# A two-layer graph network on one core: a fourth buffer for the streamed weight, the identity in a borrowed tile, the scale folded into a weight product, and one pair of input loads asked for a stage later

## The chip, the cores and the metric

The kernel runs on one NeuronCore of a Trainium2 chip. The core has five engines that run side by side and are synchronised by semaphores only: TensorE (PE in the profile, with its weight loads as PEld), VectorE (DVE), ScalarE (ACT), GpSimd (POOL) and SyncE (SP). SP computes nothing; it issues DMA transfers, one after the other, in the order in which the program lists them. The metric is device time in microseconds (us) for one execution; shown is the median of several runs.

## The reference, cut to what matters

There are 32 graphs ("batches") of 512 nodes with 512 features, in float32. For each batch two layers are applied:

```python
# layer 0
h = relu(layernorm(x))
agg = (adj @ h) / max(rowsum(adj), 1e-6)
x = x + relu(concat([h, agg]) @ W.T)
# layer 1
h = relu(layernorm(x))
q, k = split(h @ Wqk);  v = h @ Wv
agg = adj @ (k * mask[:, None])
w = (1 / sqrt(512)) * mask * rowsum(q * agg)
x = x + softmax(w over the nodes)[:, None] * v
```

Every one of the large products is 512x512x512. W, Wqk and Wv are the same for all batches.

## The kernel before, in words

**Products.** Every 512x512 product is cut into 2x2 blocks of 256x256 and done by the Strassen-Winograd scheme: seven block products instead of eight, with sums and differences of blocks made beforehand by DVE (`left_sums`, `right_sums`) and afterwards by DVE and ACT out of PSUM (`finish`, `copy`). `ORDER` (L82) lists the order of the seven block products. `product` (L118) is a generator: it gives control back after every group of matmuls, so that other work can be issued between the groups.

**Stages.** Layer 1's score needs only q . (A k), so the kernel forms M = Wq Wk^T once and multiplies h M by A (mask h). W's halves are W1, for h, and W2, for the aggregate. For each batch i the main loop (L851) runs four stages on PE:

- O, `layer0_out(i)`, 14 steps: h W1 plus A (h W2). Step 2j is the W1 term of the j-th block product, step 2j+1 its adjacency term.
- TV, `layer1_tv(i-1)`, 14 steps: the product of the previous batch's h1 with the packed weight `mv` (M and Wv side by side), in two levels of the block scheme.
- U, `layer1_u(i)`, 7 steps: the adjacency times the masked h1.
- Y, `layer0_y(i+1)`, 7 steps: h W2 of the next batch.

**Order of the other work.** The whole order is written by hand: a `Plan` says after which step of a stage a function is issued (`p.at(step, function)`), and `run` (L167) walks through the steps. Each engine then works off its own instructions strictly in this order. SP does the same with its DMA issues: a transfer that has to wait for a buffer or for another transfer holds back everything that is behind it in SP's list.

**W1's slots.** `wide` holds W2's blocks and h; W1's seven block sums don't fit beside them and lie in DRAM (`dw`). `Stream.load` (L406) brings one of them, 256 KB, into a slot of the pool `w1` (three slots, L408), and each is read by one step of O. In before three loads are asked for at step 0 of U (L959) and the other four at steps 1, 3, 5 and 7 of O (L859); a load in O waits until PE has read the slot that it takes over.

**The fronts.** For each batch, two batches ahead, x and adj are loaded in halves into the tag `n`, which has two slots in all (`half_tile`, L199). `FrontH.load` loads a half of x, `stats` (DVE), `variance` (DVE and POOL), `shift` (DVE) and `write` (ACT, then SP) normalise it and write it to DRAM (`dhT`), and `to.read` reads it back in another order (`shT`) for a transpose on DVE. `FrontA` does the same with adj (`sum` on ACT for the row sums, `degrees` on DVE, `write` on ACT and SP to `daT`, `to.read` as `saT`, `turn` on DVE). The slots are shared: the x of batch 4 can be loaded only when the adj of batch 3 has been scaled and written out of them. From batch 3 on, x of the batch after next is asked for in U (L984) and Y (L1032). The first batches have an order of their own: x of batch 4 is asked for in steps 5 and 6 of Y(2) (L1029, L1030).

**Scale and mask.** `mask_keep` (L787) makes two tiles out of the transposed node mask: `mraw`, the mask, and `mcol`, the mask times 1/sqrt(512). `factor` (L337, POOL) multiplies the row sums of adj by `mcol`, and the score is multiplied by that (`scores`, L543). `place` (L810, ACT) copies the blocks of M and of Wv into `mv`.

**The identity.** PE transposes with an identity matrix in a tile of its own (`identity`, L218, 128x128). `late` (L688) is a tile with 6272 columns that the start uses for Wq, Wk and the mask, in its first 5120 columns, and whose slot later holds `h1T`.

Of the kernel before, what the change touches and what calls it, by code (L numbers as in the profile page):

```python
# [11 lines left out]
F32 = mybir.dt.float32  # L12
AF = mybir.ActivationFunctionType
ALU = mybir.AluOpType
AX = mybir.AxisListType

P = 128
# [5 lines left out]
def kernel(  # L23
# [35 lines left out]
    nc = tc.nc  # L59
    B, N, F = x.shape  # L60
    C = N // P
    H = F // 2
# [36 lines left out]
    def copy(o, i):  # L99
        nc.scalar.activation(o, i, AF.Copy)  # L100
# [114 lines left out]

    mhalf = const.tile([P, C], F32, name="mhalf")
    nc.vector.memset(mhalf, -0.5)
    identity = const.tile([P, P], F32, name="identity")  # L218
    make_identity(nc, identity)

    X, AT_, DEG, W, Y, H1M, H1T, U, TV = ({} for _ in range(9))

# [3 lines left out]
    def load_x(b):  # L226

        t = xu_tile(f"xu_{b}")
        X[b] = t.rearrange("p (c f) -> p c f", c=C)
        U[b] = t.rearrange("p (k i f) -> p k i f", k=4, i=2)  # L230
        load_rows(X[b], x[b])
# [82 lines left out]
    class FrontA:  # L314
# [21 lines left out]

        def factor(self):  # L337
            W[self.b] = small.tile([P, C], F32, tag="wd", bufs=3, name=f"wd_{self.b}")
            nc.gpsimd.tensor_tensor(W[self.b], DEG[self.b], mcol[:, :, self.b], op=ALU.mult)

        def write(self, c):
            v = self.n[c // 2][:, c % 2, :]
# [55 lines left out]
    class Stream:  # L398
# [6 lines left out]

        def load(self):  # L406
            k = ORDER[self.n % 7]
            t = big.tile([P, 2, H], F32, tag="w1", bufs=3, name=f"w1_{self.n}")  # L408
            nc.sync.dma_start(out=t, in_=self.d[RIGHT[k]])
            self.tiles.append((k, t))  # L410
            self.n += 1
# [204 lines left out]
        else:  # L616
            nc.vector.transpose(dst[:, :, ts(h, H)].rearrange("p a (k r) -> p k a r", r=R), t)

    mcol = const.tile([P, C, B], F32, name="mcol")
    mraw = const.tile([P, C, B], F32, name="mraw")  # L620

    def in_order(t):
# [6 lines left out]
    held = {}  # L629

    def turn_chunk(src, c, name):

        p = held[name, c] = mm_tile(f"{name}_{c}").rearrange("p a f -> p (a f)")
        for k in range(C):
            nc.tensor.transpose(p[:, ts(k, P)], src[:, ts(k, P)], identity)

    def keep_chunk(dst, c, name, by=copy):
        by(
# [29 lines left out]

    def start():

        load_x(0)
        s2 = [exchange(weight_source(w0[:, F:2 * F])[8 * h:8 * h + 8], f"sw2_{h}") for h in range(2)]
        fa = FA[0] = FrontA(0)
# [11 lines left out]
            fh.load(h, room[:, 9728 + 1024 * h:9728 + 1024 * (h + 1)].rearrange("p (c f) -> p c f", c=2))  # L685
        sq = exchange(weight_source(wqk[:, 0:F]), "swq", rows16(5632))
        sk = exchange(weight_source(wqk[:, F:2 * F]), "swk", rows16(7680))
        late = big.tile([P, 7, 7, P], F32, tag="h1T", bufs=1, name="late").rearrange("p s i f -> p (s i f)")  # L688
        wqT = late[:, 0:2048].rearrange("p (c f) -> p c f", c=C)
        wkT = late[:, 2048:4096].rearrange("p (c f) -> p c f", c=C)  # L690
        mask_sb, mask_by = late[:B, 4096:4608], late[:B, 4608:5120]
# [36 lines left out]
        p = Plan()  # L728
# [56 lines left out]
                nc.tensor.transpose(m[:, c, :], mask_by[:, ts(c, P)], identity[:B, :B])  # L785

        def mask_keep():  # L787
            nc.scalar.activation(mcol, held["pmk"], AF.Copy, scale=scale)
            nc.scalar.activation(mraw, held["pmk"], AF.Copy)

        p.at(8, mask_order)
        f = F1[0] = FrontH1(0)
# [15 lines left out]
                )  # L808

        def place(d, which, src):  # L810
            copy(
                mv[:, 2 * (d // 2):2 * (d // 2) + 2, 2 * (d % 2):2 * (d % 2) + 2, which, :],
                src.rearrange("p (a b f) -> p a b f", a=2, b=2),
            )

        def outer(s):
# [31 lines left out]
    with tc.manual_schedule(engines=engines):  # L848
        weights, mvR = start()
        post = None  # L850
        for i in range(B):  # L851
# [4 lines left out]
            if i > 0:  # L856

                p = Plan()
                for n in range(4):  # L859
                    p.at(2 * n + 1, stream.load)  # L860
                right_y = right_sums(of(Y[i]))
                p.at(0, right_y[0])
                p.at(0, right_y[2])
                for k in (1, 3):
                    p.at(2 + 2 * (k // 2), FA[i].sums, k)
                    p.at(2 + 2 * (k // 2), right_y[k])
                if i == 1:
                    for k, g in enumerate(weights[4:]):
                        p.at(3 + 2 * k, g)
                    fa = FA[2]  # L870
                    for h in range(2):
                        for c in range(2):
                            p.at(2 + 2 * h + c, fa.sum, 2 * h + c)
                            p.at(8 + 2 * h + c, fa.write, 2 * h + c)
                        p.at(5 + 2 * h, fa.degrees, h)
                    FH[3] = FrontH(3)
                    p.at(12, FH[3].load, 0)
                    p.at(13, FH[3].load, 1)
                f1 = F1[i - 1]
                for k in range(4):  # L880
                    p.at(k // 2, f1.sums, k)
                if post is not None:
                    for c in range(C):
                        p.at(2 + c, post.apply, c)
                    p.at(3, post.add_x1, 0)
                    p.at(5, post.add_x1, 1)
                    p.at(9, post.store, 0)
                    p.at(11, post.store, 1)
                for k in range(4):
                    p.at(2 + k, f1.inner_sums, k, 0, 7)  # L890
                if 1 < i and i + 2 < B:
                    fh = FH[i + 2]
                    for c in range(C):
                        p.at(3 + c, fh.stats, c)
                        p.at(10 + c, fh.write, c)
                    p.at(7, variance, fh.t)
                    p.at(9, shift, fh.t)
                if more:
                    th = FH[i + 1]
                    p.at(2, th.to.read, 1)  # L900
                    p.at(11, th.turn, 0)
                if 1 < i and i + 2 < B:
                    fa = FA[i + 2] = FrontA(i + 2)
                    p.at(12, fa.load, 0)
                p.at(12, f.stats, 0)
                p.at(12, f.stats, 1)
                p.at(13, variance, f.t, 0, 2)
                run(layer0_out(i, stream.take), 14, p)


                post = Post(i - 1, F1[i - 1])
                p = Plan()
                p.at(0, f.stats, 2)
                p.at(0, shift, f.t, 0, 2)
                p.at(0, f.stats, 3)
                p.at(1, variance, f.t, 2, 4)
                if last:
                    p.at(1, FA[i].factor)
                p.at(3, shift, f.t, 2, 4)
                for c in range(C):  # L920
                    p.at([2, 3, 5, 6][c], f.write, c)
                    p.at(8 + c, f.mask, c)
                p.at(1, f.keep)
                for k in range(4):
                    p.at([10, 12, 12, 12][k], f.masked_sums, k)
                if 1 < i and i + 2 < B:
                    p.at(1, fa.load, 1)
                    for h in range(2):
                        for c in range(2):
                            p.at(4 + 4 * h + 2 * c, fa.sum, 2 * h + c)  # L930
                        p.at(8 + 4 * h, fa.degrees, h)
                if i == 1:
                    fa = FA[3] = FrontA(3)
                    p.at(11, fa.load, 0)
                    p.at(13, fa.load, 1)
                    fh = FH[3]
                    for c in range(C):
                        p.at(4 + c, fh.stats, c)
                        p.at(9 + c, fh.write, c)
                    p.at(7, variance, fh.t)  # L940
                    p[9].insert(0, lambda t=fh.t: shift(t))
                if more:
                    p.at(3, th.turn, 1)
                    for k in range(4):
                        p.at(5 + k // 2, th.sums, k)
                p.at(8, f.to.read, 0)
                p.at(9, f.to.read, 1)
                for k in range(7):
                    p.at(12 + k // 4, post.recombine, k, 0, 0)
                run(layer1_tv(i - 1), 14, p)  # L950
# [3 lines left out]
            if more:  # L954
                p.at(0, f.turn, 0)
                p.at(1, f.turn, 1)
                p.at(2, FA[i + 1].to.read, 0)
                p.at(3, FA[i + 1].to.read, 1)
                for n in range(3):  # L959
                    p.at(0, stream.load)  # L960
            if i == 0:
                fh = FH[2]
# [35 lines left out]
            if more:  # L998
# [17 lines left out]
                if i == 0:  # L1016
                    for c in range(C):
                        p.at([2, 3, 4, 4][c], fh.write, c)
                    for k in range(1, 4):
                        p.at(3 + k, weights[k])  # L1020
                    FA[2] = FrontA(2)
                    p.at(5, FA[2].load, 0)
                    p.at(6, FA[2].load, 1)
                elif i == 1:
                    p.at(0, fa.degrees, 1)
                    for c in range(C):
                        p.at(2 + c, fa.write, c)
                    FH[4] = FrontH(4)
                    p.at(5, FH[4].load, 0)  # L1029
                    p.at(6, FH[4].load, 1)  # L1030
                elif i + 3 < B:
                    p.at(0, FH[i + 3].load, 1)  # L1032
                run(layer0_y(i + 1), 7, p)
# [74 lines left out]
```

## Time and profile before

| what | value |
|---|---|
| median of 7 runs | 2293.31 us (2289.42 to 2294.66) |
| the profiled execution | 2293.65 us |
| its span, first to last instruction | 2291.6 us |
| PE busy | 2247.8 us, 98% of the span |
| DVE busy | 1930.9 us, 84% |
| ACT busy | 1027.5 us, 45% |
| POOL busy | 185.8 us, 8% |
| bytes moved | 463.65 MB, 202 GB/s on average |

The profile counts a PE matmul as busy while it is in the array, so 98% says that matmuls were nearly always under way, and not how fast they ran. How fast is said by the granted clock (PEclk, 1.00 is full speed). "Idle before, releaser" is the time in which an engine had nothing under way just before an instruction, and the work whose end let that instruction start. Durations of DMA issues on SP (SPq) are those of the issue; when the data has arrived is given as the time to landing.

### The profile page before, as it was taken

How to read it: one execution, taken by the hardware profiler on the slowest of the kernel's cores; microseconds unless marked ns; L12 is line 12 of the kernel's file. 1: busy time of each engine (PE TensorE's matmuls, PEld its weight loads, DVE VectorE, ACT ScalarE, POOL GpSimd, SP SyncE). 2: the span in 40 equal slices, each digit the busy share in tenths (PEclk: the TensorE clock that was granted, in tenths of full speed). 3: DMA queues.
4: the chain of work that ended last, by engine and by line, in shares of the span. 5: the costliest groups of instructions: out<-in, count | busy, mean ns of one | idle time of the engine just before them, and what ended most of it. 6: DMA issues, size and time to landing. Idle time of an engine off the chain costs nothing.

```text
span 2291.6 us, 32519 instructions
## 1 busy us (share of the span) xinstructions
PE 2247.8 (98%) x10372; PEld 1970.1 (86%) x10372; DVE 1930.9 (84%) x3807; ACT 1027.5 (45%) x1901; POOL 185.8 (8%) x267
## 2 busy tenths in 40 slices
PE   7998999999999999999999999999999999999996
PEld 6787888888888888888888888888888888888885
DVE  6797888888888888888888888888888888888868
ACT  4454434544434454444454345444344544444332
POOL 0000000000100000100000000000000001000002
PEclk9999999999999999999999999999999999999998
DMA  9877877777878777778878777878787778777552
GB/s 220 231 215 207 214 201 202 209 221 200 215 193 210 214 217 206 212 191 210 222 205 215 202 198 211 222 197 220 191 211 210 219 204 215 190 210 209 152 138 65
DMA packets 409594, 463.65 MB, mean 202 GB/s; under 512 B 37680, under 2 KB 271152, under 8 KB 405328
## 3 DMA queue, kind: packets, MB, share of 16 engines
q1 hardware_dynamic: 400176, 428.56, 68.5%
q0 software_dynamic: 8928, 32.51, 8.3%
q8 instruction: 82, 1.34, 0.3%
q14 instruction: 88, 0.72, 0.1%
q10 hardware_dynamic: 320, 0.52, 0.1%
HBM read 293.93 MB, written 167.51 MB: 201 GB/s over the span
## 4 chain that ended last, share of the span: by engine, by line
PE 95%; DMA 2%; DVE 2%; SPq 0%; issue 0%; ACT 0%; DVEq 0%; POOL 0%; ACTq 0%
PE ptv L467 28%; PE pp_o L130 19%; PE pq_o L130 10%; PE pp_y L130 9%; PE pp_u L130 9%; PE pq_u L130 5%; PE pq_y L130 5%; PE pr_o L130 5%; PE pr_y L130 2%; PE pr_u L130 2%; DVE wide L94 1%; PE pm L805 1%; DMA a<-in_adj_dram 1%; DMA late<-in_nodemask_dram 0%; DMA w<-dw 0%; DVE tv L94 0%
## 5 line engine op out<-in xcount | busy, mean ns | idle before, releaser
L467 PE MATMUL ptv<-mv,h1T 128*128 128x256 f32 x3136 | 682.8, 379 | 1.4 <-DVE h1T L97 1.2
L467 PEld LDWEIGHTS ptv<-mv,h1T 128*128 128x128 f32 x3136 | 595.6, 190 | 83.4 <-DVE h1T L97 1.6
L94 DVE TENSOR_TENSOR tv<-tv 128x256 f32<-128x256 f32 (+1 forms) x644 | 321.6, 511 | 11.6
L100 ACT ACTIVATE tv<-ptv 128x512 f32<-128x512 f32 (+1 forms) x372 | 191.3, 541 | 285.2 <-PE ptv L467 283.8
L130 PE MATMUL pp_o<-y,aT 128*128 128x256 f32 x1024 | 241.9, 379 | 0.0
L130 PE MATMUL pp_y<-wide 128*128 128x256 f32 x1024 | 241.9, 379 | 0.0
L130 PE MATMUL pp_u<-h1m,aT 128*128 128x256 f32 x1024 | 241.9, 379 | 0.0
L130 PE MATMUL pp_o<-w,wide 128*128 128x256 f32 x992 | 234.3, 379 | 0.0
L130 PEld LDWEIGHTS pp_u<-h1m,aT 128*128 128x128 f32 x1024 | 194.6, 190 | 26.9 <-issue 0.5
L130 PEld LDWEIGHTS pp_o<-y,aT 128*128 128x128 f32 x1024 | 194.5, 190 | 26.4
L130 PEld LDWEIGHTS pp_y<-wide 128*128 128x128 f32 x1024 | 194.5, 190 | 26.3
L130 PEld LDWEIGHTS pp_o<-w,wide 128*128 128x128 f32 x992 | 188.5, 190 | 25.6
L100 ACT ACTIVATE o<-pp_o 128x512 f32<-128x512 f32 x96 | 57.3, 597 | 296.8 <-PE pp_o L130 296.8
L94 DVE TENSOR_TENSOR tv<-ptv,tv 128x512 f32<-128x512 f32 x248 | 144.7, 614 | 46.4 <-PE ptv L467 42.5
L100 ACT ACTIVATE y<-pp_y 128x512 f32<-128x512 f32 x128 | 76.3, 596 | 234.7 <-PE pp_y L130 233.4
L97 DVE TENSOR_TENSOR h1T<-h1T 128x512 f32<-128x512 f32 (+2 forms) x195 | 168.0, 875 | 1.2
L100 ACT ACTIVATE xu<-pp_u 128x512 f32<-128x512 f32 x128 | 76.4, 597 | 198.0 <-PE pp_u L130 198.0
L248 POOL TENSOR_TENSOR rstd<-rstd,mhalf 128x2 f32<-128x2 f32 (+1 forms) x96 | 78.4, 817 | 656.9 <-DVE rstd L247 656.9
L94 DVE TENSOR_TENSOR tv<-ptv,m_tv 128x512 f32<-128x512 f32 (+1 forms) x124 | 74.5, 622 | 63.9 <-PE ptv L467 62.6
L130 PE MATMUL pq_o<-w,wide 128*128 128x256 f32 x496 | 119.2, 384 | 6.9 <-DMA w<-dw 6.9
L130 PE MATMUL pq_o<-y,aT 128*128 128x256 f32 x512 | 121.8, 381 | 0.0
L130 PE MATMUL pq_y<-wide 128*128 128x256 f32 x512 | 121.0, 379 | 0.0
(112 smaller groups left out, 3173.1 us busy)
## 6 DMA issues: line engine op xcount, KB each, us to landing
w<-dw SPq DMA_DIRECT2D x217, 256.0 KB, 4.2
xu<-in_x_dram SPq DMA_DIRECT2D x128, 256.0 KB, 5.5
a<-in_adj_dram SPq DMA_DIRECT2D x256, 128.0 KB, 3.1
dh1T<-h1m SPq DMA_DIRECT2D x128, 256.0 KB, 3.1
dx<-xu SPq DMA_DIRECT2D x32, 1024.0 KB, 5.0
sh1T<-dh1T SPq DMA_DIRECT2D x256, 128.0 KB, 3.4
shT<-dhT SPq DMA_DIRECT2D x248, 128.0 KB, 4.4
daT<-a SPq DMA_DIRECT2D x124, 256.0 KB, 3.0
```

The source lines that it names most:

```text
L94: (on or nc.vector).tensor_tensor(o, a, b, op=ALU.add)
L97: (on or nc.vector).tensor_tensor(o, a, b, op=ALU.subtract)
L100: nc.scalar.activation(o, i, AF.Copy)
L130: nc.tensor.matmul(p[:, rc, :], lt[:, LEFT[k], dk, ts(rc, P)], right[:, dk, :], start=first and n == 0, stop=True, skip_group_check=True,)
L248: nc.gpsimd.tensor_tensor(rstd[:, a:b], rstd[:, a:b], mhalf[:, a:b], op=ALU.pow)
L467: nc.tensor.matmul(banks[n][:, :, ts(i, P)], left[:, LEFT[k], LEFT_IN[j], :], mvR[:, RIGHT[k], RIGHT[j], :, :], start=first and i == 0, st ...
L805: nc.tensor.matmul(m.rearrange("p a f -> p (a f)"), wqT[:, a, ts(d, P)], wkT[:, a, :], start=(a == 0), stop=(a == C - 1),)
```

## The change

Four edits go together.

1. `identity` is no longer a tile of its own; it lies in columns 5120 to 5247 of `late`, which is therefore allocated at the beginning of `start`.
2. `mcol` is gone. `factor` multiplies by the unscaled mask, and the factor 1/sqrt(512) is applied by `place` when M is copied into `mv`; `mask_keep` makes one tile instead of two.
3. The pool `w1` has four slots. Four loads are asked for at step 0 of U and three at steps 1, 3 and 5 of O. The second half of the read-back of the next h (`th.to.read(1)`) goes from step 2 to step 4 of O.
4. x of batch 4 is asked for at steps 1 and 3 of O(2), between the loads of W1, instead of steps 5 and 6 of Y(2). Its statistics go from steps 3 to 6 to steps 5 to 8 of O(2), and the variance from step 7 to step 8.

```diff
-    identity = const.tile([P, P], F32, name="identity")
-    make_identity(nc, identity)
...
-            nc.gpsimd.tensor_tensor(W[self.b], DEG[self.b], mcol[:, :, self.b], op=ALU.mult)
+            nc.gpsimd.tensor_tensor(W[self.b], DEG[self.b], mraw[:, :, self.b], op=ALU.mult)
...
-            t = big.tile([P, 2, H], F32, tag="w1", bufs=3, name=f"w1_{self.n}")
+            t = big.tile([P, 2, H], F32, tag="w1", bufs=4, name=f"w1_{self.n}")
...
-    mcol = const.tile([P, C, B], F32, name="mcol")
...
+        late = big.tile([P, 7, 7, P], F32, tag="h1T", bufs=1, name="late").rearrange("p s i f -> p (s i f)")
+        identity = held["identity"] = late[:, 5120:5248]
+        make_identity(nc, identity)
         load_x(0)
...
-            nc.scalar.activation(mcol, held["pmk"], AF.Copy, scale=scale)
-            nc.scalar.activation(mraw, held["pmk"], AF.Copy)
+            copy(mraw, held["pmk"])
...
-            copy(
+            nc.scalar.activation(
                 mv[:, 2 * (d // 2):2 * (d // 2) + 2, 2 * (d % 2):2 * (d % 2) + 2, which, :],
-                src.rearrange("p (a b f) -> p a b f", a=2, b=2),
+                src.rearrange("p (a b f) -> p a b f", a=2, b=2), AF.Copy, scale=1.0 if which else scale,
             )
...
                 p = Plan()
-                for n in range(4):
+                for n in range(3):
                     p.at(2 * n + 1, stream.load)
...
                     fh = FH[i + 2]
+                    late = 0
+                    if i == 2:
+                        late = 2
+                        p.at(1, fh.load, 0)
+                        p.at(3, fh.load, 1)
                     for c in range(C):
-                        p.at(3 + c, fh.stats, c)
+                        p.at(3 + late + c, fh.stats, c)
                         p.at(10 + c, fh.write, c)
-                    p.at(7, variance, fh.t)
+                    p.at(7 + late // 2, variance, fh.t)
                     p.at(9, shift, fh.t)
                 if more:
                     th = FH[i + 1]
-                    p.at(2, th.to.read, 1)
+                    p.at(4, th.to.read, 1)
...
-                for n in range(3):
+                for n in range(4):
                     p.at(0, stream.load)
...
                     FH[4] = FrontH(4)
-                    p.at(5, FH[4].load, 0)
-                    p.at(6, FH[4].load, 1)
```

More of the change, by code (lines that the diff above doesn't have):

```diff
@@ L634, in turn_chunk @@
         for k in range(C):
-            nc.tensor.transpose(p[:, ts(k, P)], src[:, ts(k, P)], identity)
+            nc.tensor.transpose(p[:, ts(k, P)], src[:, ts(k, P)], held["identity"])
     def keep_chunk(dst, c, name, by=copy):
@@ L687, in start @@
         sk = exchange(weight_source(wqk[:, F:2 * F]), "swk", rows16(7680))
-        late = big.tile([P, 7, 7, P], F32, tag="h1T", bufs=1, name="late").rearrange("p s i f -> p (s i f)")
         wqT = late[:, 0:2048].rearrange("p (c f) -> p c f", c=C)
```

## The prediction

> **What bounds the kernel now.** I read the page first (busy shares, granted clock), then PE's waits, then the chain of waits around the longest of them, then windows and DVE's timeline there.
>
> ```profile
> PE 2247.8 (98%) x10372; PEld 1970.1 (86%) x10372; DVE 1930.9 (84%) x3807; ACT 1027.5 (45%) x1901; POOL 185.8 (8%) x267
> PEclk9999999999999999999999999999999999999998
> ```
>
> PE is busy for 98% of the span at nearly full clock, so time can be won only where PE stands still or runs slowly. These are all of PE's waits:
>
> ```profile
> PE h L635 <- ACT h L707: 13.6, 1, 13.6
> PE pq_o L130 <- DMA w<-dw: 6.9, 1, 6.9
> PE pq_o L130 <- ACT m_o L100: 1.5, 1, 1.5
> PE ptv L467 <- DVE h1T L97: 1.2, 1, 1.2
> PE ptv L467 <- DVE xu L94: 0.2, 1, 0.2
> ```
>
> The first and third lie in the start, the last two in the last batch, the second in batch 2. PE's windows from one O to the next, of batches 1, 2 and 3, with PE busy, granted clock, DMA share and GB/s:
>
> ```profile
> 95.41:164.88 69.47, 69.47 (x322) 1.00 0.71 193
> 164.88:244.29 79.41, 72.52 (x324) 0.96 0.84 216
> 244.29:313.79 69.50, 69.50 (x323) 1.00 0.80 209
> ```
>
> A batch takes 69.5 us with PE never idle; batch 2 takes 79.41, 9.91 more, in which the 6.89 us wait is only a part. The chain through it:
>
> ```profile
> 171.95 1.58 PE pp_o L130 x8
> 173.54 8.62 DMA w<-dw
> 182.16 0.14 issue
> 182.30 6.31 PE pq_o L130 x16
> 188.60 3.45 PE pp_o L130 x16
> ```
>
> PE is done with the third block product of O(2) at 175.41 and waits until 182.30 for the fourth block of W1, whose transfer was issued at 173.54 and took 8.62 us. The next 16 matmuls take 6.31 us instead of 3.45: in 182.30 to 188.44 the granted clock is 0.57. Why the transfer is issued so late stands in SP's timeline:
>
> ```profile
> 150.42 2.33 SPq L409 DMA_DIRECT2D w<-dw  x3
> 152.80 4.35 SPq L212 DMA_DIRECT2D saT<-daT  x8
> ...
> 167.05 0.34 SPq L344 DMA_DIRECT2D daT<-a  x1
> 168.20 5.24 SPq L204 DMA_DIRECT2D n<-in_x_dram  x8
> 173.54 0.37 SPq L409 DMA_DIRECT2D w<-dw  x1
> 174.01 3.19 SPq L212 DMA_DIRECT2D shT<-dhT  x4
> 177.29 9.10 SPq L409 DMA_DIRECT2D w<-dw  x3
> ```
>
> The load takes a slot that PE frees at about 166.7 (O(2)'s first step), but on SP it stands behind eight loads of x of batch 4, which had to wait until batch 3's adj was written out (167.05) and keep SP until 173.44. The program puts this only into batch 2.
>
> **The change part by part.**
>
> *Fourth slot, four loads in U.* The block that PE waits for becomes the last of the w loads at about 152.7, 22 us before its use at 175.4; the longest landing of a w in this stretch is 8.9 us. The wait goes: -6.89. With it goes the slow clock behind it: 6.31 - 3.45 = -2.86. The remaining 0.13 is the next stage's first product group (21.29 against 21.15 elsewhere, seen in batch 1 too); I take 0 of it. Sum -9.75. Here a rule can be weighed. The Trainium skill, "TensorE: Matmul & The Clock Gate", section "What's actually happening", says that an idle array drops to half clock and comes back after a busy window of about 3.4 us. By that the slow clock would be worth an estimated 1.7 us (half of 3.4) and the sum -8.6; the row here has 2.86.
>
> *What is late next among the w loads.* Three remain in O(2), at steps 1, 3, 5, now between the x loads. A step lasts 24.17 / 14 = 1.73 us, O(2) starts at 164.88, so they are needed at steps 8, 10 and 12: 178.7, 182.2 and 185.6. SP is free after 167.4; w, four x (2.6 us), w, four x, four shT (3.2) and w then go out at about 168, 171 and 177.3, each after PE freed its slot (166.7, 170.1, 173.5). With this stretch's 8.6 us they land at 176.6, 179.6 and 185.9; with the all-over median of 4.2, four us sooner. The third is 0.3 late at worst. I take 0, since 0.75 MB of the traffic that made 8.62 then lies in front of it and has landed; bounds 0 and 0.3.
>
> *One more load in front of saT (U).* The extra w costs SP 0.4 to 0.8 us (three took 2.33), and its 256 KB at the 236 GB/s of this stretch take 1.1. In batch 2 DVE waits for saT already (2.32 and 1.48 us idle before its two transposes), so DVE starts O(2) later by s = 0.4 to 1.1. DVE's timeline here:
>
> ```profile
> 169.69 0.68 DVE L94 TENSOR_TENSOR y<-pq_y,y 128x512 f32<-128x512 f32 x1
> 170.29 0.68 DVE L94 TENSOR_TENSOR tv<-tv 128x512 f32<-128x512 f32 x1
> 170.89 1.41 DVE L97 TENSOR_TENSOR y<-y 128x512 f32<-128x512 f32 x2
> ```
>
> These y sums end at 172.30 and PE needs them at step 5, 173.52: 1.2 us of slack, which s just keeps. I take 0; bounds 0 and 3.0 (if a full landing of 4.2 came on top: 4.2 - 1.2). In batches 3 to 31 saT goes out at 293.6 to 298.2 behind daT, which waits for ACT, not for w (SP's longest wait there is 5.5 us for ACT's scaled adj), and DVE takes it at 305.87 and 307.06; with 5.7 us, the longest landing of batch 2, it is there by 303.9. Slack 3.2, cost 0.
>
> *x of batch 4 and its statistics in O(2).* The same eight loads (128 KB each), the same four statistics on DVE, two steps later. x lands by about 171 + 4.0 and 174 + 4.0; DVE comes to the statistics only at 182.5 + s, because in before it reaches them at 177.96 and five other operations (4.5 us) now stand ahead. Nothing waits on DVE. But the wait on PE was cover: DVE runs behind in O(2), and used the stall to catch up. Without it, the operation that adds `m_o` comes 22.6 + s us after the start of O; in batch 3 it comes after 18.26 (262.55 - 244.29), in batch 1 after 22.77 (118.18 - 95.41). Batch 1 is thus the nearest row for a DVE this far behind, and it took 69.47 us with no PE wait. What batch 1 doesn't have is ACT's row sum of adj at step 4 of TV. In batch 2 the adj load stands on SP behind the write-out of the normalised x, which waits for the variance: by the rows that becomes 193.6 + s to 195.3 + s for the issues, and with 3.1 us landing at 198.4 + s. ACT reaches the row sum near 196.5, so it waits about 2 us, and four evictions of PSUM and the `m_tv` copies queue behind it; `m_tv`'s first two end at 204.4 + s, and PE wants those banks at 189.05 + 10 x 1.51 = 204.15 and 204.9. So 0.2 to 0.9 us of stall. I take +0.8; bounds 0 and 4.2 (the longest wait of ACT for an adj load in the trace).
>
> *`th.to.read(1)` from step 2 to 4.* Four issues past one w load (batch 2: past a w and four x). They are read by DVE at step 3 of TV, 273.98 in batch 3, having been issued at 246.48: 27 us early. 0.
>
> *Scale, mask, identity.* One ACT operation of 0.26 us fewer at 62.6, beside 0.83 us of ACT idle at 64.4 and a PE that is busy all through 60 to 70: 0. The four copies of M keep their form (0.57 to 0.60 us), with a constant scale; 0, bounds -0.2 and +0.2. The identity is built by the same two POOL operations (0.20 and 0.28 us, done by 10.2, needed at 13.6) in columns nothing else uses: 0. `factor` reads another tile: 0.
>
> **Sum.** -9.75 + 0.8 = -8.95. The profiled execution took 2293.65 (2291.6 span and 2.05 around it), 0.34 above the median; 2293.65 - 8.95 = 2284.7, and against the median of the runs 2293.31 - 8.95 = 2284.4.
>
> **The rivals.**
>
> *A. DVE or ACT takes the place of the transfer.* Behind DVE, in O(2) or TV(1), PE waits at the top of my bounds: 3.0 + 4.2 = 7.2 left at the most, 4.5 as a middle; some clock may go with it (the 1.5 us wait at 48 was followed by a group of 3.72 instead of 3.45). For: ACT and DVE are both in order, and 84% DVE leaves little to catch up with. Against: batch 1. Time 2293.31 - 9.75 + 4.5 = 2288.1, up to 2290.8.
>
> *B. The stall only moves.* The x loads still sit between w loads; if the second pair waits for its slot (the last write of adj, 167.05, took 4.6 us to land, so until 171.7) and everything behind lands as late as the shT reads of this stretch (9.2 us), the last w arrives at 178 + 9.2 = 187.2, 1.6 late, with more if DMA is slower than before. Full price would need it 7 us later than now. Time between 2285.1 and 2293.3.
>
> *C. Slower.* The fourth w load stands ahead of saT in every U, 30 times. If it put saT back by more than the 3.2 us of slack, and then past the 5.4 us between the y sums' end (247.53) and their use at step 5 (252.9), 8.6 in all, PE would stall in every batch. With 0.6 us a batch: 29 x 0.6 = 17.4, time 2284.4 + 17.4 = 2301.8. It decides from 9 / 29 = 0.3 us a batch. Against: SP's wait for ACT there swallows an issue of 0.45 us, and DMA is at 0.66 of its time in U.
>
> **How the numbers follow.** My forecast (residue below 2 us) 0.66, A 0.18, B 0.08, C 0.08. Two runs of this kernel can't be told apart below about 0.2% (4.6 us). Faster: the forecast, two thirds of A and part of B: 0.80. Same: the rest of A and B and a little of C: 0.13. Slower: C, 0.07. The range goes from the whole excess of batch 2 recovered with 1 us of scatter, 2293.31 - 9.91 - 1 = 2282.4, to A at a residue of 5.5 us, 2289.1.
>
> **What would show it.** In the profile of the changed kernel, PE's wait for w in O(2) is gone, and no window of O(2) has a granted clock under 1.00; batch 2 takes 69.5 to 71.5; DVE waits for saT about a microsecond longer than 2.32 and 1.48 in Y(2); ACT waits for adj in TV(1) by some 2 us; batches 3 to 31 stay at 69.50. Wrong would be: a PE wait for ptv banks or y above 2 us, a w wait at steps 8 to 12, or any batch after the third longer than 69.6.

## The result and the profile after

The changed kernel takes 2286.07 us (median of 13 runs, 2284.12 to 2288.32), the kernel before 2292.38 (31 runs, 2289.42 to 2294.66). The ratio is 0.9973 with a 95% interval of 0.9965 to 0.9980, a gain of 6.3 us (4.6 to 8.0). The profiled executions are further apart: 2284.12 after, 2293.65 before, 9.5 us. The forecast was 8.95.

The page of the changed kernel, its busy shares and the granted clock:

```profile
PE 2245.8 (98%) x10372; PEld 1969.3 (86%) x10372; DVE 1930.4 (85%) x3807; ACT 1028.2 (45%) x1900; POOL 185.6 (8%) x267
PEclk9999999999999999999999999999999999999998
```

The work is the same, one ACT instruction less. PE's waits, all of them (us in total, times, longest):

```profile
PE h L632 <- ACT h L706: 13.5, 1, 13.5
PE ptv L465 <- DVE h1T L97: 1.2, 1, 1.2
PE pp_o L130 <- DMA w<-dw: 0.8, 1, 0.8
PE ptv L465 <- DVE xu L94: 0.2, 1, 0.2
PE pp_o L130 <- DVE y L97: 0.2, 1, 0.2
```

The 6.9 us for W1 are gone. Two small waits have come, both in O(2): 0.8 for W1's last block, 0.2 for the y sums. The windows from one O to the next (PE busy, clock, DMA share, GB/s), batches 1, 2 and 3:

```profile
94.78:164.17 69.39, 69.39 (x322) 1.00 0.69 190
164.17:235.37 71.20, 70.17 (x324) 1.00 0.90 242
235.37:304.87 69.50, 69.50 (x323) 1.00 0.80 210
```

Batch 2 takes 71.20 instead of 79.41, and its mean granted clock is 1.00 instead of 0.96. (Both windows end about 0.17 us after the first matmul of O(3); from start to start batch 2 takes 71.03 and 79.24.) PE's timeline of O(2) around the two waits, and SP's:

```profile
173.21 1.99 PE L130 MATMUL pp_o<-y,aT 128*128 128x256 f32 x8 [0.24 <-DVE y L97]
175.04 1.89 PE L130 MATMUL pq_o<-w,wide 128*128 128x256 f32 x8
...
186.35 1.97 PE L130 MATMUL pp_o<-w,wide 128*128 128x256 f32 x8 [0.78 <-DMA w<-dw]
188.15 1.89 PE L130 MATMUL pp_o<-y,aT 128*128 128x256 f32 x8
```

```profile
149.97 2.81 SPq L407 DMA_DIRECT2D w<-dw  x4
152.88 5.33 SPq L212 DMA_DIRECT2D saT<-daT  x8
...
168.03 0.60 SPq L407 DMA_DIRECT2D w<-dw  x1
168.68 1.94 SPq L204 DMA_DIRECT2D n<-in_x_dram  x4
171.10 0.34 SPq L407 DMA_DIRECT2D w<-dw  x1
172.00 1.72 SPq L204 DMA_DIRECT2D n<-in_x_dram  x4
173.94 4.07 SPq L212 DMA_DIRECT2D shT<-dhT  x4
178.11 0.65 SPq L407 DMA_DIRECT2D w<-dw  x1
```

The fourth block, for which PE waited before, is now the last of the four loads at 150. The fourth block's product at 175.04 follows its predecessor without a pause. The last load goes out at 178.11, behind 4.07 us in which SP is busy with the shT reads, although its slot had been free since 173; it takes 8.11 us and PE waits 0.78.

### The profile page after: what moved, and what is told of

Read it like the earlier page. It is cut to its first block, busy times and chain, and to the rows that moved or that the text cites. A ratio compares the mean times of both kernels' runs of the same rounds, so it can differ in the third digit from the quotient of the medians.

```text
span 2282.2 us, 32577 instructions
## 1 busy us (share of the span) xinstructions
PE 2245.8 (98%) x10372; PEld 1969.3 (86%) x10372; DVE 1930.4 (85%) x3807; ACT 1028.2 (45%) x1900; POOL 185.6 (8%) x267
## 4 chain that ended last, share of the span: by engine, by line
PE 96%; DVE 3%; DMA 1%; issue 0%; POOL 0%; SPq 0%; ACT 0%; DVEq 0%
PE ptv L465 29%; PE pp_o L130 19%; PE pq_o L130 10%; PE pp_y L130 9%; PE pp_u L130 9%; PE pq_y L130 5%; PE pr_o L130 5%; PE pq_u L130 5%; PE pr_u L130 2%; PE pr_y L130 2%; DVE wide L94 1%; PE pm L803 1%; DMA w<-dw 1%; DVE tv L94 1%; DMA xu<-in_x_dram 0%
## 5 line engine op out<-in xcount | busy, mean ns | idle before, releaser
L130 PE MATMUL pq_u<-h1m,aT 128*128 128x256 f32 x512 | 120.9, 379 | 0.0
```

The costliest lines, as they stand in the source:

```text
L130: nc.tensor.matmul(p[:, rc, :], lt[:, LEFT[k], dk, ts(rc, P)], right[:, dk, :], start=first and n == 0, stop=True, skip_group_check=True,)
```

## Experiments

**1. Which part does it.** Three kernels with a part of the change each.

Tiles and scale alone (three slots, all loads as before):

```diff
-    identity = const.tile([P, P], F32, name="identity")
+        identity = held["identity"] = late[:, 5120:5248]
...
-            nc.scalar.activation(mcol, held["pmk"], AF.Copy, scale=scale)
-            nc.scalar.activation(mraw, held["pmk"], AF.Copy)
+            copy(mraw, held["pmk"])
```

> The kernel before with the identity in the borrowed tile and the scale in the copy of M, three slots and all loads as before. Theory 1: no difference, within 0.1% of before, PE's wait for w in batch 2 between 5 and 7 us. Rival (the freed tile changes the start): the first TV stage starts 0.5 us or more earlier or later and the time moves with it.

Measured: 2291.25 against 2292.10, ratio 0.9997 (0.9988 to 1.0006): no difference. PE waits 7.17 us for W1 in its profile. This part makes room and no time.

The slots alone (the changed kernel with x of batch 4 back in Y(2)):

```diff
-                    late = 0
-                    if i == 2:
-                        late = 2
-                        p.at(1, fh.load, 0)
-                        p.at(3, fh.load, 1)
...
+                    p.at(5, FH[4].load, 0)
+                    p.at(6, FH[4].load, 1)
```

> The changed kernel with x of batch 4 asked for in steps 5 and 6 of Y(2) again; the fourth slot, the tiles and the scale stay. Theory 1 (SP's order holds the load back): four blocks of W1 are there, but the fifth is now the one behind the eight x loads; it is issued at about 173.5 and lands after 8.6 us at 182, 3.5 to 4 us after step 8 wants it. PE waits 3 to 4 us at step 8, the clock may or may not fall behind it; gain over before 3 to 6.5 us. Rival (three slots are the cause): the wait is gone whatever stands on SP, gain as of the changed kernel, 6 us.

Measured: 2289.01 against 2292.10, ratio 0.9985 (0.9976 to 0.9994). Neither theory had the place of the wait; the gain of 3.1 by the medians is at the lower end of theory 1's 3 to 6.5. SP's timeline, and PE's at the one wait for W1:

```profile
168.77 5.01 SPq L204 DMA_DIRECT2D n<-in_x_dram  x8
173.88 0.84 SPq L407 DMA_DIRECT2D w<-dw  x2
174.82 4.16 SPq L212 DMA_DIRECT2D shT<-dhT  x4
179.09 0.58 SPq L407 DMA_DIRECT2D w<-dw  x1
```

```profile
188.00 1.97 PE L130 MATMUL pp_o<-w,wide 128*128 128x256 f32 x8 [1.67 <-DMA w<-dw]
189.80 1.89 PE L130 MATMUL pp_o<-y,aT 128*128 128x256 f32 x8
```

The fifth block goes out at 173.88, as theory 1 had it, but lands after 4.9 us and not 8.6, before step 8 wants it at 179.26. Late is the seventh, behind the shT reads, by 1.67 us. The trace is of an execution of 2285.87, 3.1 us under this kernel's median, so at the median more is lost than it shows.

x of batch 4 alone (three slots):

```diff
+                    late = 0
+                    if i == 2:
+                        late = 2
+                        p.at(1, fh.load, 0)
+                        p.at(3, fh.load, 1)
...
-                    p.at(5, FH[4].load, 0)
-                    p.at(6, FH[4].load, 1)
```

> The kernel before with x of batch 4 asked for at steps 1 and 3 of O(2), its statistics two steps later, and nothing else. Theory 1 (SP's order): the fourth block goes out at about 168 and lands in time or up to 1 us late, the fifth stands behind four x loads and the shT reads, goes out at about 174 and lands 0.5 to 4 us late at step 8; gain over before 4 to 9 us. Rival (the slots are what counts): PE still waits 5 us or more in O(2), gain below 3.

Measured: 2289.52 against 2292.10, ratio 0.9983 (0.9975 to 0.9992). By the medians the gain is 2.6, by the ratio 3.9 (1.8 to 5.7), so it lies at or below the lower end of theory 1's 4 to 9. The place of the wait is theory 1's: the fourth block is in time, PE waits 2.84 us at step 8 for the fifth, which went out at 173.38 behind four x loads and the shT reads. The wait is not all of the loss: batch 2 still takes 4.8 us more than 69.50 in this trace, and 1.8 of them are slow clock. PE's window of the 16 matmuls behind the wait:

```profile
182.01:187.22 5.21, 5.21 (x16) 0.67 0.95 277
```

They take 5.21 us instead of 3.45, at a granted clock of 0.67. In these traces each of the two parts alone leaves a longer wait for W1 than both together, for which experiment 5 has 0.78 and none.

**2. Slots or order.** The kernel before with three slots, and in O(2) x of batch 4 and the shT reads asked for behind all the loads of W1, the statistics and the write-out moved back with them:

```diff
+                    if i == 2:
+                        late = 4
+                        p.at(7, fh.load, 0)
+                        p.at(7, fh.load, 1)
...
-                    p.at(2, th.to.read, 1)
+                    p.at(7 if i == 2 else 2, th.to.read, 1)
```

> The kernel before with three slots, and in O(2) alone x of batch 4 and the shT reads asked for behind all four loads of W1 (step 7), its statistics four steps later, the write-out at step 13. Theory 1 (the order on SP makes the wait, not the number of slots): no wait for w in O(2) above 0.5 us; what is late next is the write-out of x and the adj load behind it, so that ACT waits 3 to 6 us for adj in TV(1) and PE waits 0 to 4 us for PSUM. Rival (three slots are too few): PE still waits 2 us or more for a block of W1.

Measured: 2285.88 in a single run, beside 2290.99 for the median of before, which ran alongside. SP's timeline:

```profile
166.41 10.68 SPq L409 DMA_DIRECT2D w<-dw  x4
177.14 4.54 SPq L204 DMA_DIRECT2D n<-in_x_dram  x8
```

There is no wait for W1 at all with three slots. O(2) runs through, and a shorter stall stands one stage later. The waits of PE in TV(1) in PE's timeline:

```profile
188.66 6.50 PE L467 MATMUL ptv<-mv,h1T 128*128 128x256 f32 x28
196.72 9.33 PE L467 MATMUL ptv<-mv,h1T 128*128 128x256 f32 x42 [1.56 <-ACT tv L100]
206.42 6.31 PE L467 MATMUL ptv<-mv,h1T 128*128 128x256 f32 x28 [0.37 <-ACT m_tv L100]
```

So three slots are enough when the order on SP is another. The slots alone took most of the wait away too (1.67 was left): before's long wait needed both, a fourth load that had to wait for a slot and eight x loads ahead of it on SP. The price of this order is on ACT, which stands 10.65 us for the late statistics before it normalises x, and only then comes to the evictions. Its wait for adj is 2.12, less than the 3 to 6 that were expected; PE's two waits for ACT, 1.9 together, lie within the 0 to 4.

**3. The two waits that are left.** The four shT reads at step 6 instead of 4, behind the last load of W1:

```diff
-                    p.at(4, th.to.read, 1)
+                    p.at(6, th.to.read, 1)
```

> The changed kernel with the second read-back of the next h (four shT reads) asked for at step 6 of O instead of step 4, that is, behind the last load of W1. Theory 1 (the last load is late because SP is held by the shT reads, 4.07 us in front of it): it goes out at about 174 instead of 178.1, lands by 182, and PE's 0.78 us wait at step 12 is gone; batch 2 at 70.2 instead of 71.09, time 0.9 below the changed kernel. Rival (the DMA engines are full and the load lands late wherever it stands): the wait stays above 0.5.

And with it the fourth load in U behind the saT reads:

```diff
                 for n in range(4):
-                    p.at(0, stream.load)
+                    p.at(0 if n < 3 else 4, stream.load)
```

> The same, and the fourth load of W1 in U at step 4, behind the saT reads, instead of step 0. Theory 1 (the load in front of saT puts DVE back by 0.86 us): DVE's first wait for saT falls from 3.87 to about 3 us or less, the y sums end before PE wants them, PE has no wait in batch 2 and the batch takes 69.5 to 69.8; time 1.2 to 1.6 below the changed kernel. Rival (saT's delay came from elsewhere): the 0.24 us wait for y stays.

Measured: 2284.22, ratio 0.9972 (0.9961 to 0.9984), and 2283.81, ratio 0.9970 (0.9959 to 0.9980), with before at 2290.99. By the ratios neither can be told from the changed kernel's 0.9973. There is one trace of each. With the reads later, the last load goes out at 174.26 and the wait for it is gone, though the load is no faster: it lands after 8.4 us, against 8.1 behind the reads. The wait for y is 0.97 here, so batch 2 takes 70.75 and not the 70.2 expected, and in TV(1) PE waits 0.66 for DVE. With the fourth load behind saT as well, DVE's longest wait for saT is 2.7 us instead of 3.9 and PE has no wait in O(2). This fits theory 1 both times, but a second trace of the changed kernel (experiment 5) has neither wait either, so that the moves took them away is not shown. PE's waits in that kernel:

```profile
PE h L632 <- ACT h L706: 13.5, 1, 13.5
PE ptv L465 <- DVE h1T L97: 1.2, 1, 1.2
PE ptv L465 <- DVE xu L440: 0.3, 1, 0.3
PE ptv L465 <- DVE xu L94: 0.2, 1, 0.2
PE pp_y L130 <- ACT y L100: 0.2, 1, 0.2
```

From the start of TV(0) to the start of TV(1) it takes 69.90, a little over the 69.5 to 69.8 expected, and the next round 70.06: DVE, which runs behind, now holds PE by 0.3 us in TV(1).

**4. The residue that was forecast.** The prediction charged 0.8 us for ACT, which waits in TV(1) for batch 4's adj and holds back the evictions. Here that load is asked for later still, in TV(1):

```diff
+                    if i > 2:
                         p.at(12, fa.load, 0)
...
+                    if i == 2:
+                        p.at(1, fa.load, 0)
                     p.at(1, fa.load, 1)
```

> The changed kernel with the first half of batch 4's adj asked for at step 1 of TV(1), behind the keeping of x, instead of step 12 of O(2). Theory 1 (the residue that was forecast: ACT waits for adj in TV(1) and holds back the evictions of PSUM): ACT's wait for adj grows from 1.35 to 4 us or more and PE waits 1.5 us or more for PSUM in TV(1), which the changed kernel does not. Rival (the eight PSUM banks have more slack than I reckoned): ACT waits longer and PE still doesn't wait.

Measured: 2285.91 in a single run. ACT's timeline in the changed kernel and in this one:

```profile
198.69 0.63 ACT L328 ACTIVATE a<-a 128x512 f32<-128x512 f32 x1 [1.35 <-DMA a<-in_adj_dram]
203.04 1.85 ACT L100 ACTIVATE m_tv<-ptv 128x512 f32<-128x512 f32 x4
```

```profile
201.61 0.63 ACT L328 ACTIVATE a<-a 128x512 f32<-128x512 f32 x1 [4.95 <-DMA a<-in_adj_dram]
205.96 1.85 ACT L100 ACTIVATE m_tv<-ptv 128x512 f32<-128x512 f32 x4
```

ACT waits 4.95 us, as theory 1 said, but PE waits only 0.34 and 0.45 in TV(1), less than the 1.5 expected, and in the changed kernel not at all. The mechanism is there, with more slack in front of it than was reckoned: 3.6 us more of ACT's wait cost PE 0.8. Part of this slack is PE's own lateness. O(2), the same as in the changed kernel, has waits of 0.54 for y and 1.89 for W1's last block in this execution, and TV(1) begins 27.1 us after O(2) instead of the 24.17 that O(2) takes without a wait.

**5. Why the medians are closer than the profiles.** The kernel before three more times, the changed kernel once more, unchanged:

> The kernel before once more, unchanged, for a second profile of it. The medians of the two kernels differ by 6.3 us, the two profiled executions by 9.5. Theory 1 (batch 2's wait for w and the slow clock behind it differ from execution to execution): this profile shows an excess of batch 2 over 69.50 other than 9.88 us, somewhere in 5 to 10. Rival (the wait is the same in every execution and the start differs): the excess is again 9.9 within 0.3, and the moment at which the first TV stage starts moves by up to 4 us instead.

> The kernel before, unchanged, a third profile. Open is why the medians differ by 6.3 us while the first two profiled executions differ by 9.5. Theory 1 (batch 2's stall differs between executions of the kernel before): an execution of 2289 us or less has a batch 2 of 76 or less, one of 2293 has 79 to 80. Theory 2 (the start differs): batch 2 stays at 79.4 within 0.3, and the start of the first TV stage moves (118.9 and 119.4 so far) by as much as the time does.

> The same once more, a fourth profile, with the same expectations.

> The changed kernel, unchanged, a second profile; its first was of its fastest execution (2284.12). Theory 1 (the waits that are left in O(2) differ between executions): at the median of 2286 or above, PE's wait for the last block of W1 is longer than 0.78, 1.5 to 3.5 us, as in the kernel with the adj load later, which had 1.89; batch 2 72 to 74. Theory 2 (the start or the end differ): batch 2 stays at 71.1 within 0.3.

Measured, with the stalls in PE's timeline; "batch 2" is from the start of TV(0) to the start of TV(1), "next" from there to TV(2), "rest" is the time less these two:

| kernel | time of the profiled execution | waits in O(2) | batch 2 | next | rest |
|---|---|---|---|---|---|
| before | 2293.65 | w 6.89 | 79.38 | 69.50 | 2144.8 |
| before | 2293.28 | w 1.16, 5.91 | 79.55 | 69.50 | 2144.2 |
| before | 2294.81 | w 8.12 | 80.82 | 69.50 | 2144.5 |
| before | 2292.94 | y 0.40, w 5.95, 0.20 | 78.79 | 69.50 | 2144.7 |
| tiles and scale alone | 2293.83 | w 7.17 | 79.46 | 69.50 | 2144.9 |
| x alone | 2288.44 | w 2.84 | 74.27 | 69.50 | 2144.7 |
| slots alone | 2285.87 | y 0.59, w 1.67 | 72.92 | 69.50 | 2143.5 |
| after | 2284.12 | y 0.24, w 0.78 | 71.09 | 69.50 | 2143.5 |
| after | 2284.26 | none | 69.90 | 70.08 | 2144.3 |
| adj later | 2285.91 | y 0.54, w 1.89 | 72.42 | 70.83 | 2142.7 |
| three slots, x behind W1 | 2285.88 | none | 69.84 | 72.26 | 2143.8 |
| reads later | 2284.22 | y 0.97 | 70.75 | 70.43 | 2143.0 |
| reads and fourth load later | 2283.81 | none | 69.90 | 70.06 | 2143.8 |

The stall of batch 2 does differ between executions of one kernel, in length (6 to 8 us) and in place: the second trace of the kernel before has it split over two blocks, at steps 6 and 8:

```profile
176.06 1.97 PE L130 MATMUL pq_o<-w,wide 128*128 128x256 f32 x8 [1.16 <-DMA w<-dw]
177.86 1.89 PE L130 MATMUL pq_o<-y,aT 128*128 128x256 f32 x8
185.66 3.75 PE L130 MATMUL pp_o<-w,wide 128*128 128x256 f32 x8 [5.91 <-DMA w<-dw]
189.20 2.54 PE L130 MATMUL pp_o<-y,aT 128*128 128x256 f32 x8
```

The landing times of W1's loads show what these differences go with. In O(2) and every later O, GpSimd issues a pair of transfers of its own, 512 KB each, the second 1.2 us behind the first (`tv<-dx`, which add x to the result). The pair in the first and in the second trace of before:

```profile
172.05 2.10 POOL L573 DMA_DIRECT2D tv<-dx  x2 [3.55 <-ACT tv L566]
172.58 2.09 POOL L573 DMA_DIRECT2D tv<-dx  x2 [3.54 <-ACT tv L566]
```

In the first trace the fourth block's load goes out at 173.54, 0.3 us behind the second transfer of the pair, and takes 8.62 us. In the second it goes out at 172.97, 0.8 us ahead of that transfer, and takes 2.96. Over the changed kernel's first trace, from batch 2 on, the 30 loads that went out within 5 us behind the pair took 7.6 to 9.8 us, the other 180 took 2.5 to 5.6. The shT reads by themselves don't go with it: in the first trace of before 28 loads went out less than 4 us behind them with no pair under way, and took 2.8 to 4.1. No run moves the pair, so that it causes the slow landing is not shown.

Over these thirteen executions the rest moves by 2.2 us and the two batches together by 10.3; they decide the time. Of the expectations, the second trace's excess of 10.05 still fitted the rival's 9.9 within 0.3; the third trace then refutes a fixed stall of 79.4 within 0.3 (80.82), and the second of the changed kernel refutes a fixed 71.1 (69.90); the fast execution of before and the slow one of after that theory 1 speaks of were not caught. The four traces of before all lie at 2292.9 or above and the two of after at 2284.3 or below, so no trace shows an execution of before near 2289 or one of after near 2288. That these have a shorter stall, and a longer one, would fit and is not shown. Why the medians differ by 6.3 and the traces by 9.5 stays open.

## Why the prediction was right, point by point

**What bounds the kernel, and the stall.** Right: PE's only mendable wait was that of batch 2, and the load came late by SP's order. Experiment 2 shows it without the fourth slot. That the load then took 8.62 us to land goes with GpSimd's pair of transfers (experiment 5), which the prediction did not reckon with.

**The price of the stall, 9.75.** Batch 2's excess over 69.50 was 9.3 to 11.3 in four executions of before. In the prediction's own trace it is 79.24 - 69.50 = 9.74 from start to start, so the sum of 9.75 leaves nothing over; the 9.91 came from a window that ended 0.17 late. The clock's part, 2.86, can now be set against the length of the wait. The 16 matmuls that follow take 3.45 us at full clock. After a wait of 0.78 or 1.67 us they took 3.53, after 2.84 us 5.21, after 5.91 5.92, after 5.95 5.13, after 6.89 6.14 (the prediction's 6.31 has 0.17 of the last matmul's end in it), after 7.17 5.86 and after 8.12 5.93. So the loss is 0.1 after waits of up to 1.67 and 1.7 to 2.7 from 2.84 on, and it does not grow with the wait. The Trainium skill's "TensorE: Matmul & The Clock Gate", section "What's actually happening", puts the fall of the clock after an idle window of about 3.4 us, and its warm-up gave the 8.6 in the prediction. The losses after 2.84 and 5.95 us (1.8 and 1.7) are near that estimate, the other four (2.4 to 2.7) nearer the row; and here 2.84 us of idle time were enough for the clock to fall.

**The last load of W1, taken as 0 with bounds 0 and 0.3.** Mis-sized: 0.78 in one execution of the changed kernel, 0 in the other, 1.89 in experiment 4. By the prediction's own list a wait for w at steps 8 to 12 was a sign of being wrong, and this is one, at step 12. Two steps failed. The shT reads in front of the load were to take 3.2 us on SP, and took 4.07. And the traffic ahead of it was to have landed: the four shT reads landed at 184.1 to 185.6, shortly before the load at 186.2, and GpSimd's pair had gone out at 172.9 and 174.1; so the load took 8.11. In experiment 3, ahead of the reads, it took 8.4 and 9.5 and was in time only because it went out earlier.

**saT and the y sums, taken as 0.** Mis-sized in the first trace. DVE's first wait for saT grew from 2.32 to 3.87, the y sums ended at 173.16, and PE waited 0.24 for them (0.97 at most in the other kernels with this order). Counted from the start of O(2), which is what PE goes by, they ended after 8.99 us instead of 7.42, 1.57 later, more than the s of 0.4 to 1.1: SP spent 2.81 us on four loads instead of 2.33 on three, and 5.33 on the saT reads instead of 4.35. Nor was the slack of 1.2 us a property of the kernel. In the four traces of before the sums ended 7.0 to 9.1 us after the start of O(2), and in the last of them PE waited 0.40 for y with three loads; in the second trace of the changed kernel they ended after 8.1, without a wait. The bounds, 0 to 3.0, held.

**ACT and adj in TV(1), +0.8.** The largest residue in the sum, and not there: ACT waited 1.35 for adj (2 forecast) in both traces, PE did not wait. `m_tv`'s copies began at 203.04; the prediction had the first two end at 204.4 + s, 205.3 with s at 0.86, and they ended at 204.1. In the first trace TV(1) also began 0.8 later than reckoned (189.88 against 189.05), after PE's waits in O(2); in the second PE had none there and still did not wait for ACT. Experiment 4 shows the mechanism at a larger delay.

**DVE behind, with batch 1 as the row.** Right in kind, taken too lightly in size. The addition of `m_o` came 24.2 us after the start of O(2) in the first trace (188.39 - 164.17) and 23.4 in the second; 22.6 + s, 23.0 to 23.7, was forecast. In the first PE took no harm in TV(1), but it had lost 1.5 us in O(2) itself. In the second, with nothing lost in O(2), it waited 0.32 in TV(1) for DVE, and 0.30 and 0.66 in the kernels of experiment 3. Batch 1, the row for no harm, had 22.77.

**Sum.** The residue was 1.6 us in one execution and 1.0 over two batches in the other (0.6 of it in TV(1), the rest in TV(0), ahead of O(2)), against 0.8 forecast. That the size is near is partly luck: ACT's 0.8 did not come, and the terms taken as 0 (w, y, DVE) did. It is near in the traces alone: the medians differ by 6.3, 2.6 less than the forecast of 8.95, and where the rest is stays open. Tiles and scale cost nothing by themselves; the later read-back, charged with 0, has no run of its own, and it is behind these reads that the last load stands. Batches 4 to 31 stayed at 69.50. Rival A was right in kind (DVE takes over in part) and 0.2 to 0.3 us in size in these two traces. Rival B's mechanism, the last block behind the shT reads, came in one of them, at half its lowest price. Rival C did not come: in the changed kernel no U or Y of the later batches shows a wait.

## What to carry to other kernels

When an engine is busy for 98% of the time, list all of its waits and price each with the slow stretch behind it; here one late transfer of 256 KB cost 6.9 us of waiting and 2.9 us of slow clock. A load that is late is first a question of what stands ahead of it on the issuing queue: with the same three buffers and another order the wait was gone. Then look at what else is under way when it goes out, other engines' transfers too. And a stall covers other lateness; before it is taken out, look along each in-order engine for what would be late next, and reckon that slack from the start of the work that needs it and from more than one trace: here one kernel's y sums ended 7.0 to 9.1 us after the start of O(2).

## What the runs showed of the hardware that was not expected

A wait of PE of 2.84 us was followed by 16 matmuls in 5.21 us instead of 3.45, at a granted clock of 0.67; waits of 0.78 and 1.67 us were followed by 3.53. Somewhere between these the clock began to fall. Beyond that the loss did not follow the length of the wait: 1.7 us after 5.95, 2.5 after 5.91.

The same transfer in the same place of SP's list landed in very different times. The fourth block of W1, behind eight x loads and just ahead of the shT reads, took 8.6, 3.0, 9.9 and 7.1 us in the four traces of before. The long times go with GpSimd's pair of 512 KB transfers under way: in the changed kernel 7.6 to 9.8 us for a 256 KB load just behind the pair, 2.5 to 5.6 otherwise. That the pair is the cause is not tested.
